# Four-layer hybrid network on one core: the last image's residual rows stay in SBUF, its positions and first norm go by halves, and 1/std is spread two chunks at a time

## The chip, the cores and the metric

The kernel runs on one core of a Trainium2 chip, in fp32. A core has five engines that run their own instruction streams in order: TensorE (PE, with its weight loads shown apart as PEld), VectorE (DVE), ScalarE (ACT), GpSimd (POOL) and SyncE (SP). They meet at semaphores. DMAs are issued from the queues of SP, ACT and POOL. The metric is the time of one execution on the device in microseconds; the median of several runs is compared.

## The reference

Four images of 96 channels and 64×64 pixels pass through four residual layers. Cut to what matters, with `_gn` a norm over groups of three channels, `_ln_t` a norm over the 96 channels of a pixel:

```python
x = x + layer0(_gn(x))        # norm, projection to 192+192 (x and gate z), 3x3 depthwise conv, silu,
                              # state-space scan over the 4096 pixels in four directions (rows, columns,
                              # each forwards and backwards), 16 states per channel;
                              # y = sum of the four; norm over 192; y*z; projection to 96
x = x + layer1(_gn(x))        # deformable 3x3 conv: a 3x3 conv gives 18 offsets and 9 masks per pixel,
                              # 9 taps are sampled bilinearly at base+offset, times the mask, then 96x96 each
t = t + fourier(_ln_t(t))     # 96 -> 192, relu, FFT over 4096 pixels, diagonal complex product, relu,
                              # inverse FFT, 192 -> 96
t = t + ffn(_ln_t(t))         # 96 -> 384 -> 96 with values rounded to short floats
t = t + linear_attention(_ln_t(t))
t = t + ffn(_ln_t(t))
```

## The kernel before

Images are worked on in order, and different layers of different images overlap. `Layer0.scan` is a list of 1536 scan units, 384 per image, in an order written out by hand. A unit covers 8 channels × 16 states on 128 partitions and 1024 pixels: ACT makes `da`, PE spreads the input into `db` (L1020), DVE multiplies and scans (L1034, L1042), POOL multiplies by `bc` (L1051), PE folds 128 rows into 32 (L1070). SP loads `du`, `bc` and stores `y`; ACT's queue loads `da`.

Between two units, the program is filled up with steps of two Python generators, called streams. `ends` holds `l0.first` and `l0.before(b)` (the inputs of the scans of each image) and then `l23.image(b)`, which is layers 2 and 3 of an image. `middle` holds, image by image, `l0.behind(b)` (out norm, gate and projection, giving x1) and `l1.image(b)` (layer 1, giving x2). Every step declares a cost per engine in microseconds; `Clock.has_room` lets a step in where the planned ends of the engines are not too far ahead, and `pipe` runs several chains of steps side by side, each when its tags (`takes`, `frees`) and PSUM banks (`has_bank`) allow. This happens while the program is built. On the chip each engine executes its instructions in the order in which the planner emitted them. Once the scan is over, `alone()` advances the planner's time by itself. `go()` steps both streams, `middle` first until the flag `sampling_last` is set, `ends` first from then on.

The parts that the change touches, for image b:

- `behind(b)`, L1092: for each pair of 512-pixel chunks from the last to the first, the sum of the column directions (`yta`, `ytc`, loaded transposed by halves of the image, L1112) and of the row directions, by POOL (L1134); centring and variance on PE; inverse root; spread of 1/std; gate by POOL (L1180); projection; x added (L1189) and x1 stored to DRAM.
- `offsets`, L1237: x1 loaded, `wom` loaded, group statistics (eight `bn_stats`, L448, then an aggregate and a small matmul), the normed image written by ACT, and copied by POOL into a padded tile `pad` (L1262); then 8 chunks, each with nine matmuls for the offsets (`po`, L1278), four transposes of the pixels (`pt`, L1295), copies (`pix`, `om`) and eight DMAs of 96 KB into a DRAM table (L1310) in which a row holds the four neighbours of a position.
- `positions`, L1319: loads `base`, then about 14 DVE operations of 288 or 576 columns give the row index `idx` and the four weights `wt` for all 288 × 128 taps.
- `sample`, L1366: 288 gathers (POOL, L1383), three to a tile `g`; they are weighted and summed by DVE (L1402, L1403) in the last image and by ACT (L1395) in the others; transposed (L1416), copied to `st` (L1424), multiplied by nine weight matrices (`pd`, L1432), x1 added (L1437), x2 stored to DRAM.
- `l23.image(b)`, L1819: loads x2 as `t`, and the Fourier layer begins with `normed` (L1603): `centred` (L470; chain per chunk, variance rows gathered in one bank, four rows per half), `inv_sqrt_steps`, and per chunk `spread` (L523), a matmul that copies one row of 1/std to all partitions, and a DVE product (L1613).

For the last image, layers 2 and 3 run halves of the image side by side where they can.

The last of these, the spread, reads:

```python
row = self.ident[:, j : j + 1].to_broadcast([128, 128])
self.nc.tensor.matmul(pb, lhsT=row, rhs=rstd, start=True, stop=True)
```

## Time and profile before

| what | us |
|---|---|
| median of three runs (8467.96 to 8479.75) | 8472.4 |
| the profiled execution | 8455.38 |
| its span, first to last instruction | 8453.6 |
| first and last scan on DVE start | 183.7, 7416.3 |
| last image: first gather starts | 7590.32 |
| last image: last row of x2 added, ends | 8036.3 |
| last image: first matmul of the Fourier layer | 8076.07 |
| image 2's output stored | 7905.2 |

The profiled execution is one of its own, 0.2% below the median of the runs. Times inside it are microseconds from the first instruction. The mean granted TensorE clock is 0.793 of full speed. Until 7418 the scan runs, with the other layers of earlier images between its units; what follows is the last image's way through the rest, beside the end of image 2. In a row of the timeline the bracket at the end gives the idle time of that engine ahead of the instruction and what ended it. A group's row gives its busy time, the mean of one, and the idle time before its instructions.

### The profile page before, as it was taken

To read this page: it belongs to the slowest core of one execution; us is meant where nothing else is said; L and a number is where in the kernel's file an instruction comes from. 1 tells how busy PE (TensorE), PEld (TensorE's weight loads), DVE (VectorE), ACT (ScalarE), POOL (GpSimd) and SP (SyncE) were. 2 spreads that over 40 slices of the span, in tenths; PEclk is the share of its full clock that TensorE was granted. 3 is DMA by queue.
4 is the path that set the end of the run, shared out by engine and by line. 5 is a ranking of instruction groups with operands and counts; after the bars stand their busy time and mean duration, and the time that the engine had idled before them with its cause. 6 is when DMAs were issued, how large, how long until landed. Compare 5 with 4: busy or idle time off the path is not lost.

```text
span 8453.6 us, 96209 instructions
## 1 busy us (share of the span) xinstructions
PE 6424.4 (76%) x31848; PEld 2772.6 (33%) x31848; DVE 6826.4 (81%) x5122; ACT 4914.8 (58%) x8979; POOL 5621.2 (66%) x4308
## 2 busy tenths in 40 slices
PE   6765787678766777977767889777788777797587
PEld 2211221112222223321222555222455232464273
DVE  2799889987789898779888898898898988838714
ACT  5665566555567777855566677645576876333224
POOL 1566566665568888856578898766798997627700
PEclk8776787678767778977667898786798787898698
DMA  3676678877679888877788999776899897744410
GB/s 98 169 209 186 166 190 214 204 186 188 171 205 241 233 235 220 230 187 198 194 216 233 236 237 245 184 177 175 224 239 235 216 228 188 187 111 138 142 60 17
DMA packets 773926, 1608.27 MB, mean 190 GB/s; under 512 B 264082, under 2 KB 355758, under 8 KB 771223
## 3 DMA queue, kind: packets, MB, share of 16 engines
q10 hardware_dynamic: 244224, 843.17, 39.2%
q1 hardware_dynamic: 455478, 532.37, 24.4%
q0 software_dynamic: 73728, 226.57, 10.1%
q8 instruction: 256, 4.19, 0.2%
q14 instruction: 240, 1.96, 0.1%
HBM read 1345.43 MB, written 256.29 MB: 189 GB/s over the span
## 4 chain that ended last, share of the span: by engine, by line
PE 32%; DVE 26%; DMA 12%; POOL 11%; issue 9%; ACT 8%; SPq 2%; ACTq 1%; DVEq 0%; POOLq 0%
DVE da L1042 12%; POOL da L1051 7%; DVE db L1034 7%; PE pc L763 3%; DMA da<-de 3%; PE py L1070 3%; PE ps L1416 3%; PE f L1510 3%; POOL g L1383 3%; PE pd L1432 2%; PE db L1020 2%; ACT g L1395 2%; ACT da L1014 2%; DMA du<-du 1%; PE h L1551 1%
## 5 line engine op out<-in xcount | busy, mean ns | idle before, releaser
L1051 POOL TENSOR_TENSOR da<-da,bc 128x1024 f32<-128x1024 f32 x1536 | 3664.1, 2387 | 351.6 <-DVE da L1042 233.3
L1042 DVE TENSOR_TENSOR_SCAN da<-da,st,db 128x1024 f32<-128x1024 f32 x1152 | 2701.1, 2345 | 124.1 <-ACT da L1014 12.8
L1034 DVE TENSOR_TENSOR db<-db,bc 128x1024 f32<-128x1024 f32 x1536 | 1865.4, 1214 | 614.7 <-PE db L1020 613.1
L1014 ACT ACTIVATE da<-da,w_al 128x1024 f32<-128x1024 f32 x1536 | 1737.7, 1146 | 405.7 <-DMA da<-de 166.9
L1383 POOL DMA_INDIRECT g<-table,idx x1152 | 1206.8, 1048 | 360.2 <-issue 178.7
L1020 PE MATMUL db<-du,rep 24*128 24x512 bf16 x3072 | 683.7, 450 | 774.4 <-DVE da L1042 729.0
L1070 PE MATMUL py<-da,w_fold 128*32 128x512 f32 x6144 | 1091.8, 784 | 43.6 <-issue 25.2
L1395 ACT ACTIVATE g<-g,wt 128x96 f32<-128x96 f32 x3456 | 964.0, 365 | 107.1 <-DMA g<-table,idx 18.4
L1042 DVE TENSOR_TENSOR_SCAN da<-da,db 128x1024 f32<-128x1024 f32 x384 | 877.0, 2284 | 54.7 <-ACT da L1014 19.6
L1416 PE MATMUL ps<-w_ident,g 128*96 128x128 f32 x3744 | 680.7, 325 | 252.3 <-issue 107.6
L1020 PEld LDWEIGHTS <-rep 24*128 24x128 bf16 x3072 | 147.3, 93 | 1839.2 <-DVE da L1042 1164.6
L851 POOL TENSOR_TENSOR lw<-lw,w 128x512 f32<-128x512 f32 x192 | 244.0, 1271 | 700.5 <-DVE w L849 667.8
L1416 PEld LDWEIGHTS ps<-w_ident,g 128*96 128x96 f32 x3744 | 483.5, 144 | 601.3 <-issue 178.9
L1049 POOL COPY st<-da 128x1 f32<-128x1 f32 x1152 | 232.2, 202 | 674.1 <-DVE da L1042 655.8
L763 PE MATMUL pc<-pad,wc 96*128 96x512 f32 x1152 | 576.3, 636 | 7.0 <-DVE rl L853 5.3
L1424 ACT COPY st<-ps 96x384 f32<-96x384 f32 x384 | 180.2, 472 | 572.3 <-PE ps L1416 533.8
L882 PE MATMUL pr<-ex,w_ident 128*128 128x512 f32 x384 | 311.2, 904 | 125.5 <-DVE ex L866 53.5
L1432 PE MATMUL pd<-st,wdc 96*128 96x256 f32 x1152 | 323.7, 434 | 12.7 <-DVE rl L853 6.0
L763 PEld LDWEIGHTS pc<-pad,wc 96*128 96x128 f32 x1152 | 217.9, 200 | 318.6 <-issue 303.5
L840 PE MATMUL pd<-xd,w_dtw 103*64 103x512 f32 (+1 forms) x512 | 273.4, 799 | 47.0 <-DVE rl L853 15.6
L1070 PEld LDWEIGHTS py<-da,w_fold 128*32 128x32 f32 x6144 | 158.1, 124 | 381.1 <-issue 300.3
L1432 PEld LDWEIGHTS pd<-st,wdc 96*128 96x128 f32 x1152 | 243.2, 219 | 104.2 <-issue 39.5
(259 smaller groups left out, 8631.4 us busy)
## 6 DMA issues: line engine op xcount, KB each, us to landing
da<-de ACTq DMA_DIRECT2D x1536, 512.0 KB
du<-du SPq DMA_DIRECT2D x1536, 96.0 KB
bc<-bcd SPq DMA_DIRECT2D x128, 512.0 KB
y<-yb SPq DMA_DIRECT2D x384, 128.0 KB
de<-rl SPq DMA_DIRECT2D x128, 256.0 KB
m<-in_dft SPq DMA_DIRECT2D x128, 256.0 KB
ad<-y ACTq DMA_DIRECT2D x192, 128.0 KB
table<-pix SPq DMA_DIRECT2D x256, 96.0 KB
```

What stands on the lines that cost most here:

```text
L763: nc.tensor.matmul(pp, lhsT=wc[:, q, g * 128 : (g + 1) * 128], rhs=pad[:, r0 + dy : r0 + dy + NR, dx : dx + W], start=(q == 0), stop=(q == 8),
L882: nc.tensor.matmul(pr, lhsT=net.ident, rhs=ex, start=True, stop=False)
L1014: self.net.nc.scalar.activation(u.da, u.da, AF.Exp, scale=self.al[:, a : a + 1])
L1020: self.net.nc.tensor.matmul(db[:, h, :], lhsT=self.rep[64 * u.q + 32 * h : 64 * u.q + 32 * h + 24], rhs=u.du[64 * u.q + 32 * h : 64 * u.q ...
L1034: self.net.nc.vector.tensor_mul(u.db, u.db, u.bc[:, 0, :])
L1042: nc.vector.tensor_tensor_scan(u.along(u.hh), u.along(u.da), u.along(u.db), first, ALU.mult, ALU.add)
L1051: self.net.nc.gpsimd.tensor_mul(u.hh, u.hh, u.bc[:, 1, :])
L1070: nc.tensor.matmul(py[p0 : p0 + 32], lhsT=self.fold[:, u.i, :], rhs=hc[:, h * CH : (h + 1) * CH], start=u.sums["add"] is None and u.i == 0 ...
L1383: nc.gpsimd.indirect_dma_start(out=g[:, k, :], out_offset=None, in_=self.tables[b % 2], in_offset=bass.IndirectOffsetOnAxis(ap=idx[:, n : ...
L1395: nc.scalar.activation(pixel, pixel, AF.Identity, scale=wt[:, n, c : c + 1])
L1416: nc.tensor.matmul(pt[:, k, :], lhsT=g[:, k, c * C : (c + 1) * C], rhs=net.ident, is_transpose=True, start=(c == 0), stop=(c == corners - 1),)
L1432: nc.tensor.matmul(po, lhsT=wdc[:, k, :], rhs=st[:, k, :], start=(k == 0), stop=(k == 8))
```

## The change

1. For the last image, x1 is a tile `x` in SBUF (pool `l1x`). It is loaded with the whole input image; `behind` adds to it in place and takes `bn_stats` of each chunk there. Neither the store of x1 nor its loads remain for this image. The transposed y is loaded by quarters of the image. In the very last pair of chunks, the sums and gate products are on DVE and no longer on POOL.
2. For all images, `offsets` lets ACT write the padded tile itself. The table comes first, in four chains `table(jj)` of 16 image rows each: 16 small matmuls against the identity from `pad`, two copies, eight DMAs of 192 KB. The eight chunks follow without transposes. For the last image the buffers are taken from the scan's ring of tiles (`ring`, `wide`).
3. `positions` takes a range of the taps. For the last image it runs twice on halves: the first after chunk 3 and the second as the first chain of `sample`; taps of the second half take the tag `half`.
4. `sample` of the last image adds to `x` in place, has `st` twice, and marks chunks in `net.arrived`; no x2 is stored or loaded.
5. The first norm of the last image's Fourier layer runs by halves, and its chains take `x{j}`, so that they can be emitted as the chunks arrive.
6. `spread` contracts over the 32 rows that hold the wanted one. `normed` and `normed_rows` issue the spreads of two chunks together.
7. `go()` tries `middle` first, and `ends` only if that one cannot step, whenever no scan unit paces the program (after the scan's end above all) and `sampling_last` is not yet set.

```diff
-            if chain.new and not net.has_bank():
+            if chain.new and not net.has_bank(int(chain.new)):
...
-            if not all(free[tag] > 0 for tag in chain.takes):
+            if not all(free.get(tag, net.arrived.get(tag, 0)) > 0 for tag in chain.takes):
...
-    def group_norm_stats(self, x, pool, key, stats):
+    def group_norm_stats(self, x, pool, key, stats, st=None):
 
         nc = self.nc
-        st = pool.tile([C, NCH, 6], F32, name=f"gnst{key}", tag="gnst")
-        for j in range(NCH):
-            nc.vector.bn_stats(st[:, j, :], x[:, j * CH : (j + 1) * CH])
-            if j % 2:
-                yield cost(dve=1.4)
+        if st is None:
+            st = pool.tile([C, NCH, 6], F32, name=f"gnst{key}", tag="gnst")
+            for j in range(NCH):
+                nc.vector.bn_stats(st[:, j, :], x[:, j * CH : (j + 1) * CH])
+                if j % 2:
...
-            yield wait(new=True, takes="sq")
+            yield wait(new=True, takes=f"sq x{j}" if arriving else "sq")
...
     def spread(self, rstd, j, n, key):
 
         pb = self.mm(f"lnb{key}_{j}")
-        row = self.ident[:, j : j + 1].to_broadcast([128, 128])
-        self.nc.tensor.matmul(pb, lhsT=row, rhs=rstd, start=True, stop=True)
+        k = slice(j - j % 32, j - j % 32 + 32)
+        row = self.ident[k, j : j + 1].to_broadcast([32, 128])
+        self.nc.tensor.matmul(pb, lhsT=row, rhs=rstd[k], start=True, stop=True)
         return pb[:n]
...
-                yield cost(pe=1.2, holds=1)
-                r = rows(pad, j)
-                nc.vector.tensor_mul(r, r, as_rows(pb))
-                yield cost(dve=0.7)
-                nc.scalar.activation(r, r, AF.Identity, scale=net.vec(V_ING, C), bias=net.vec(V_INB, C))
-                yield cost(act=0.8)
-
-            yield from pipe(self.net, (chain(j) for j in range(NCH)), 3)
+                yield wait(new=2)
+                pbs = [net.spread(rs, 32 * ((j + i) % 4) + (j + i) // 4, C, f"0_{b}") for i in range(2)]
+                yield cost(pe=1.2, holds=2)
+                for i in range(2):
+                    r = rows(pad, j + i)
+                    nc.vector.tensor_mul(r, r, as_rows(pbs[i]))
+                    yield cost(dve=0.7, holds=1 - i)
+                    nc.scalar.activation(r, r, AF.Identity, scale=net.vec(V_ING, C), bias=net.vec(V_INB, C))
+                    yield cost(act=0.8, holds=1 - i)
+
+            yield from pipe(self.net, (chain(j) for j in range(0, NCH, 2)), 2)
 
...
+    def ring(self, name, n, dtype=F32):
+
+        return self.sp.tile([128, T], dtype, name=name, tag="da", bufs=12)[:, :n]
+
+    def wide(self, name):
+        return self.sp.tile([128, 2, T], F32, name=name, tag="bc").rearrange("p s t -> p (s t)")
...
-                    ytc = big.tile([D2, W, H // 2], F32, name=f"ytc{b}_{h0}", tag="ytc")
+                rows = H // 2 if x1 is None else H // 4
+                if (j0 + HB) * NR % rows == 0:
+
+                    h0 = (j0 + HB) * NR - rows
+                    yta = big.tile([128, W, rows], F32, name=f"yta{b}_{h0}", tag="yta")
+                    ytc = big.tile([D2, W, rows], F32, name=f"ytc{b}_{h0}", tag="ytc")
                     for yt, c0 in ((yta, 0), (ytc, 128)):
                         src = self.y_d[b][3][c0 : c0 + yt.shape[0]].rearrange("c (w h) -> c w h", h=H)
-                        nc.sync.dma_start(yt, src[:, :, h0 : h0 + H // 2])
+                        nc.sync.dma_start(yt, src[:, :, h0 : h0 + rows])
                     yta_v, ytc_v = (t.rearrange("p w h -> p h w") for t in (yta, ytc))
                     yield wait(4.0)
                 while not all((b, 2, j * CH // T) in self.summed for j in range(j0, j0 + HB)):
                     yield BLOCKED
+                ends = b == B - 1 and j0 == 0
                 ca = big.tile([128, HB, CH], F32, name=f"ca{b}_{j0}", tag="ca")
                 cc = big.tile([D2, HB, CH], F32, name=f"cc{b}_{j0}", tag="cc")
                 net.hold(1)
...
-                    yield cost(pool=3.1, new=True)
+                        (nc.vector if ends else nc.gpsimd).tensor_add(y, y, yt[:, rs, :])
+                    yield cost(pool=3.1 * (not ends), dve=1.4 * ends, new=True)
                     for g, (o, c0, n) in enumerate(((ca, 0, 128), (cc, 128, D2))):
...
-                    yield cost(pool=2.6, new=True)
+                        (nc.vector if ends else nc.gpsimd).tensor_mul(o[:, i, :], o[:, i, :], z)
+                    if x1 is None:
+                        xr = op.tile([C, CH], F32, name=f"xr{b}_{j}", tag="xr")
+                        nc.sync.dma_start(xr, ins["x"][b][:, cs])
+                    else:
+                        xr = x1[:, cs]
+                    yield cost(pool=2.6 * (not ends), dve=1.4 * ends, new=True)
                     po = net.mm(f"po{b}_{j}")
                     nc.tensor.matmul(po, lhsT=wo_a, rhs=ca[:, i, :], start=True, stop=False)
...
                     yield cost(pe=1.3, holds=1)
                     nc.vector.tensor_add(xr, po[:C], xr)
-                    yield cost(dve=0.7)
-                    nc.sync.dma_start(self.x1[b][:, cs], xr)
-                    yield NOTHING
+                    if x1 is None:
+                        yield cost(dve=0.7)
+                        nc.sync.dma_start(self.x1[b][:, cs], xr)
+                        yield NOTHING
+                    else:
+                        nc.vector.bn_stats(st[:, j, :], xr)
+                        yield cost(dve=1.4)
...
+    def image(self, b, l0, ctx):
+
+        net = self.net
+        tc, nc = net.tc, net.nc
+        last = b == B - 1
+        if not last:
+            yield from l0.behind(b)
+        with ExitStack() as own:
+            if last:
+                kept = ctx.enter_context(tc.tile_pool(name=f"l1x{b}", bufs=1, side="right"))
+                x = kept.tile([C, L], F32, name=f"x1_{b}", tag="x")
+                st = kept.tile([C, NCH, 6], F32, name=f"gnst1_{b}", tag="gnst")
+                yield from l0.behind(b, x, st)
+            ix = own.enter_context(tc.tile_pool(name=f"l1i{b}", bufs=1, side="right"))
             idx = ix.tile([128, 288], U32, name=f"idx{b}", tag="idx")
             wt = ix.tile([128, 288, 4], F32, name=f"wt{b}", tag="wt")
...
+                def place_of(h):
+
+                    yield wait(takes=f"om{h}" if h == 0 else "")
+                    key = f"{b}_{h}"
...
+                    yield from self.positions(key, lambda name, *_: parts[name], om, base, idx, wt, 16 * h, 16)
+                    if h:
+                        net.arrived["half"] = 1
+
+                yield from self.offsets(b, x, st, om, place_of, l0)
+            else:
...
+            net.sampling_last = b == B - 1
+            if b == B - 1:
+                net.last_image = x
+            yield from self.sample(b, x, idx, wt, l0, place_of if last else None)
+        net.sampled.add(b)
...
+
             def filled(j):
-                cs = slice(j * CH, (j + 1) * CH)
-                nc.scalar.activation(x[:, cs], x[:, cs], AF.Identity, scale=rstd, bias=nmr)
+                nc.scalar.activation(Layer0.rows(pad, j), plain_rows(x, j), AF.Identity, scale=rstd, bias=nmr)
                 yield cost(act=0.8)
-                nc.gpsimd.tensor_copy(
-                    pad[:, 1 + j * NR : 1 + (j + 1) * NR, 1 : 1 + W],
-                    x[:, cs].rearrange("p (h w) -> p h w", w=W),
-                )
-                yield cost(pool=0.7)
-
-            yield from pipe(self.net, (filled(j) for j in range(NCH)), 2)
...
+            def table(jj):
+
+                yield wait(new=True, takes="pix")
+                if place_of is None:
+                    pix = pre.tile([128, 8, C], F32, name=f"pix{b}_{jj}", tag="pix")
+                else:
+                    pix = l0.ring(f"pix{b}_{jj}", 8 * C).rearrange("p (q c) -> p q c", c=C)
+                for h in range(2):
+                    pt = net.mm(f"pt{b}_{jj}_{h}")[:, : 4 * C].rearrange("p (q c) -> p q c", c=C)
+                    for q in range(4):
+                        for r in range(2):
+                            row = pad[:, 1 + 16 * jj + 8 * h + 2 * q + r, 1 : 1 + W]
+                            nc.tensor.matmul(
+                                pt[64 * r : 64 * r + 64, q, :],
+                                lhsT=row,
+                                rhs=net.ident[:C, :C],
+                                start=True,
+                                stop=True,
+                            )
+                    nc.scalar.copy(pix[:, 4 * h : 4 * h + 4, :], pt)
+                    yield cost(pe=0.9, act=0.5, new=h == 0)
+                for q in range(4):
+                    dy, dx = divmod(q, 2)
+                    for r in range(2):
+                        y0 = 2 + 16 * jj + r - dy
+                        dst = v[y0 : y0 + 15 : 2, 2 - dx : 2 - dx + W, q * C : (q + 1) * C]
+                        nc.sync.dma_start(dst.rearrange("t w d -> w t d"), pix[64 * r : 64 * r + 64])
+                yield wait(frees="pix")
 
             def chunk(j):
                 r0 = j * NR
+                yield wait(new=True, takes="po")
...
+            def chains():
+                for jj in range(NCH // 2):
+                    yield table(jj)
+                for j in range(NCH):
+                    yield chunk(j)
+                    if place_of is not None and j == 3:
+                        yield place_of(0)
+
+            yield from pipe(net, chains(), 4, every=-99, oc=min(deep, 2), pix=deep, po=min(deep, 2), om0=-3, om1=-3)
...
-                yield wait(takes="g")
+                yield wait(takes="g half" if last and t >= 16 else "g")
...
-                xr = gp.tile([C, 256], F32, name=f"xr1_{b}_{j}", tag="xr")
-                nc.sync.dma_start(xr, self.x1[b][:, cs])
+                if last:
+                    xr = xo = x[:, cs]
+                else:
...
-                nc.sync.dma_start(self.x2[b][:, cs], xo)
+                if not last:
+                    nc.sync.dma_start(self.x2[b][:, cs], xo)
+                elif j % 2:
+                    net.arrived[f"x{j // 2}"] = 1
...
-            yield from pipe(self.net, chains, 8, g=6, st=1, xo=1)
+            def chains():
+                if last:
+                    yield place_of(1)
+                for t in range(4 * NCH):
+                    for k0 in (0, 3, 6):
+                        yield taps(t, k0)
+
...
-                yield from normed(net, t, tl, f"2_{b}", pool)
+                if b == B - 1:
+                    for r in range(2):
+                        yield from normed(net, t, tl, f"2_{b}_{r}", pool, (r,), True)
+                else:
+                    yield from normed(net, t, tl, f"2_{b}", pool)
             tv = tl.rearrange("c (n1 n2) -> c n1 n2", n2=64)
...
+            if clock.own is not None and not net.sampling_last:
+                return any(stream.step() for stream in streams[::-1])
             return any([stream.step() for stream in (streams if net.sampling_last else streams[::-1])])
```

## Prediction

> **What bounds the kernel now.** I read the page's totals, the chain and the groups first. (Group rows: line, engine, operation, out<-in, count | busy us, mean ns | idle before, releaser.)
>
> ```profile
> span 8453.6 us, 96209 instructions
> ...
> PE 6424.4 (76%) x31848; PEld 2772.6 (33%) x31848; DVE 6826.4 (81%) x5122; ACT 4914.8 (58%) x8979; POOL 5621.2 (66%) x4308
> ...
> PE 32%; DVE 26%; DMA 12%; POOL 11%; issue 9%; ACT 8%; SPq 2%; ACTq 1%; DVEq 0%; POOLq 0%
> ...
> L1042 DVE TENSOR_TENSOR_SCAN da<-da,st,db 128x1024 f32<-128x1024 f32 x1152 | 2701.1, 2345 | 124.1 <-ACT da L1014 12.8
> L1034 DVE TENSOR_TENSOR db<-db,bc 128x1024 f32<-128x1024 f32 x1536 | 1865.4, 1214 | 614.7 <-PE db L1020 613.1
> ...
> L1383 POOL DMA_INDIRECT g<-table,idx x1152 | 1206.8, 1048 | 360.2 <-issue 178.7
> L1020 PE MATMUL db<-du,rep 24*128 24x512 bf16 x3072 | 683.7, 450 | 774.4 <-DVE da L1042 729.0
> ```
>
> No engine bounds the whole: the chain is spread over five. So I split the span by the timeline: 1536 scan units on DVE, 183.7 to 7418; then a tail of 1035 us. In the scan phase the two DVE operations need 1.21+2.35 = 3.6 us a unit, yet it advances at 4.5 to 4.9: other work and stalls. The tail by windows (busy us and count of PE, weight loads, DVE, ACT, POOL; granted clock; DMA share; GB/s):
>
> ```profile
> 7441.00:7481.00 40.00, 39.99 (x308) 25.46 (x308) 19.93 (x28) 9.33 (x15) 11.29 (x8) 1.00 0.19 53
> 7500.00:7590.00 90.00, 85.40 (x917) 67.12 (x915) 9.45 (x20) 36.22 (x72) 4.88 (x8) 0.96 0.53 121
> 7590.00:8025.00 435.00, 275.09 (x1031) 161.49 (x1030) 332.54 (x463) 114.03 (x233) 347.32 (x290) 0.74 0.49 144
> 8036.00:8076.00 40.00, 24.15 (x48) 8.58 (x48) 7.64 (x12) 10.19 (x19) 0.00 (x0) 0.74 0.17 42
> ```
>
> The last image's gathers cannot start before 7590.32, though PE is 95% busy before: that is image 2's Fourier layer, which nobody waits for yet. During sampling POOL is the fullest (347 of 435). In the last row nothing is full: a serial chain.
>
> **The change, part by part.** Sums are against the profiled execution, 8455.4 (span 8453.6); the runs' median 8472.4 lies 17.0 above it, which I add at the end.
>
> (a) Scan phase, images 0 to 2. The position arithmetic heads DVE's queue and waits for its base, whose load stands on SP behind the table's DMAs (the timelines of SP and DVE; columns: start, us, engine, instruction):
>
> ```profile
> 2375.50 5.23 SPq L1310 DMA_DIRECT2D table<-pix  x8
> ...
> 2383.00 0.35 SPq L393 DMA_DIRECT2D w_base<-in_base  x1
> ...
> 2386.28 0.76 DVE L1334 TENSOR_TENSOR pos<-om,w_base 128x576 f32<-128x576 f32 x1 [15.87 <-DMA w_base<-in_base]
> ```
>
> The same operation waits 12.68 us at 4235.70 (there a `du` load of the same queue is named, but the base is issued at 4232.54) and 10.39 at 5981.00: 38.9 in all. In the new order the table is issued 10 to 20 units ahead, so some 3.5 us of latency stays (SP 2383.00 to DVE 2386.28): 3×3.5 = 10.5, gain 28. The wait goes where? ACT's and PE's work for later units runs ahead meanwhile, so not all of the 28 need arrive. Against it: a table DMA now carries twice the bytes, 32 per image at the same total, and eight come together. With SP held 10.91 us by eight 96 KB issues at 4212.26, a batch costs at best nothing extra and at worst another 10.9; four batches in three images, bounds 0 and +131. I take +10, near the lower end: the bytes are equal. Image 3's transposed y now comes in four pairs of loads, not two:
>
> ```profile
> L1112 SPq DMA_DIRECT2D ytc<-y x8: 7970/12757/15796, 1604.8 to 7300.4; - x8
> ```
>
> (min/median/max ns). After such an issue the gap between scans was 6.9 to 20.9 us where 3.6 to 4.6 is normal. A quarter has the same number of packets at half the size, so SP is held as long; of four, one falls beside the last scan unit: one more stall, +10 (0 to +30). The whole x of image 3 (1.5 MB) is loaded there too, in place of eight small loads; a load of that size took 8.73 us at 8038, with nothing waiting for it here. ACT now fills the pad itself, 8×0.61 us of POOL less per image, off the path; the 64 small transposing matmuls for 32 (0.246 us each, before) add at most 8 us of PE per image, under a scan that DVE paces. The two streams' order moves by up to 12 units late in the scan, which reshuffles every small stall; I allow ±30. Sum −8, from −38 to +25 plus the 131 treated below as a rival.
>
> (b) Scan end to x1, 7441 to 7481: POOL's adds 4×1.55 and products 4×1.33, 11.5 us, become DVE's, 8×0.68 = 5.4 by the nearest product of 512 columns. Two chunks go side by side, so half of the 6.1 saved, 3, is on the chain; but PE is full (39.99 of 40), and image 2's matmuls stand between. I take 1.5 (0 to 5). Then the store and load of x1 (2.07), the weights behind them (8.92 DMA) and eight statistics (4.85), 16 us on the chain before the aggregate at 7497.4, go: x is in SBUF, statistics are taken per chunk, and the weights, first needed by the chunks, load beside the aggregate and the fill. Behind the aggregate, PE's queue held Fourier matmuls until 7509.4; now the chain's own come sooner. Pad filled 13 us earlier altogether, (b) included (8 to 16).
>
> (c) Pad to first gather, 7517.9 to 7590.3 = 72.4. Before: 64 table issues paced by PE and SP, 7528.4 to 7575.2, then the whole position arithmetic (7577 to 7589.5) behind the last chunk. Now: 32 issues of twice the size from deeper buffers, placed ahead of the chunks; the DMA engines were 0.73 busy over the 47 us, so they need at least 33 and take at most 43, from about 7508. The first positions follow chunk 3 and lie under these writes; the second half does too. Pad filled ≈7505, first table DMA 7508, first gather 7541 to 7551 plus a landing: ≈7547. Gain of (b) and (c) together 43 (33 to 52). Its price: image 2's Fourier, with 8 of 12 frequency blocks still to do, is pushed into sampling, some 66 us of PE.
>
> (d) Sampling, 434 us. PE has room, 435−275 = 160 us (the 66 at clock 0.96 are some 85 at the 0.74 of this row), but not at its start (31.46 of the first 36 already), where the whole push falls. The new conditions (half of the positions, chunk arrived) are tested while the program is built; on the chip they leave an order of instructions: the norm's centring stands in PE's queue behind the `pd` that it reads, the next triple's transposes stand behind it, and after six gather buffers POOL waits for those. DVE and POOL meet here: with DVE busy 20.6 to 23.4 us, 24 gathers took 34 to 35.5 us; with 32 to 34.7 they took 36.8 to 40. So a DVE us costs 0.2 to 0.4 us. New in this stretch: about 12 us of DVE of the pushed work and 5 of the first half of the norm (five to six operations of 0.7): 17×0.3 = 5; POOL's memset of the norm tile, 3.5; a few late PE answers in the first 90 gathers, 5. Sum +14 (3 to 40).
> A gather took 0.95 alone and up to 3.4 beside a DVE product. The Trainium skill ("SBUF — State Buffer", section on the two separate sides) holds that DVE and GpSimd share an exclusive port lock, so that the loser waits the whole operation out; by that rule the 17 us would cost up to 17 instead of 5, which speaks against loading DVE here. The windows' slope decides for me.
>
> (e) From the last sampled row to the Fourier layer, 39.8 us of plain chain:
>
> ```profile
> 8036.32 1.66 DMA x<-xo
> ...
> 8038.11 8.73 DMA t<-x
> 8046.88 7.02 PE lnc L485 x8
> ...
> 8065.56 9.65 PE lnb L527 x16
> ...
> 8076.07 3.94 PE h L1551 x50
> ```
>
> Store and load, 10.6, vanish. Of the norm's two halves the first (centring, variance, 4 us of root, spreads) lies under the sampling; the second's centring is done as chunks arrive but for the last one: about 2.5 centring, 1 variance, 4.1 root, 4 spreads and a product of 0.7, some 13 to 16 left. Gain 25 (20 to 28).
>
> (f) Spreads two chunks side by side: each took 0.593 at full clock and a pair 32 rows high may overlap, as L1020's 24-row pairs do (3072×0.450 = 1382 us in 683.7 busy). The three later norms spend 8.99, 4.29+3.67 and 8.83 us in spreads; pairs leave DVE's 0.68 product as the pace, 8×0.68 = 5.4 for 8.9. Gain 8 (0 to 14): 3.5+2+3.5 less a little.
> Against it stands the skill's "TensorEngine Tiling (Array Packing)", Key Properties: changing the tiling mode drains TensorE. No row here prices a drain; if each pair paid a few tenths, the 8 would shrink to about nothing.
>
> Sum: −8−43+14−25−8 = −70: profiled 8385, and with the 17 the median is **8402**.
>
> **Rivals.** B, *more*: the scan phase keeps its 28 without the two tens, sampling hides nearly everything, the ends come at their better bounds: −28−43+3−28−14 = −110, 8362. For it: DVE and PE are light in the last 130 us of sampling (DVE 20 to 23 of 35). Against: PE is full where the push falls.
> C, *sampling gives it back*: gathers that start 43 us sooner wait for PE's late transposes, or the sampling ends with image 2 still running: +45 in place of +14, so −39, 8433. For it: 31.46 of 36 us of PE busy at the start, and 66 more. Against: only the six gather buffers couple the two.
> D, *slower*: the doubled table DMAs hold up the scan's loads. SP issues in order, du, bc and de stand behind a batch on it, and the scan unit waits for them; if each of the 12 batches holds SP for twice 10.91 us and the scan waits that long, the 131 come in place of the 10: −70+121 = +51, 8523. It decides from 72 us of scan loss beyond (a)'s. For it: L1034's idle and the 13 us `ytc` issues, which did stop the scan. Against: equal bytes, and beside the batch at 4212.26 the scans went on at 4214.27 and 4218.25 until the base stopped them.
> E, *does not do what it says*: the planner's budgets keep the priority and the early half norm from moving anything, and only the removed copies and the base count: −8−16 (b) −10.6 (e) = −35, 8437. Against: the new program's order has half the norm ahead of the last gathers.
>
> **How the numbers follow.** Chances: forecast 0.50, B 0.16, C 0.16, D 0.10, E 0.08. A measurement of this kernel tells about 0.2%, 17 us. Adding the spreads of the terms as independent (30, 9, 18, 4, 7) gives ±37, so the forecast alone is 8365 to 8440. To leave no more than 2 in 10 out, the range takes in B, C and E with half of their own spread, 8350 to 8455; D stays outside. All but D centre on clearly faster; the upper edges of C and E reach within 17 us of before: faster 0.84, same 0.06, slower 0.10.
>
> **What would show it.** First gather some 130 us after the last scan's end (174 before); waits for w_base under 4 us on DVE before `pos`; at most 435+40 us from first to last gather; Fourier's `h` within 16 us of the last `xo`; spread groups under 6 us per eight. Wrong: the last scan unit later than 7450 (D), gathers still starting over 160 us after it (E), or sampling above 475 us (C).

## The result, and the profile after

The changed kernel is slower: 8538.8 us (median of 7 runs, 8520.2 to 8552.9) against 8485.3 for the kernel before in 7 runs beside and before it (8468.0 to 8507.1), a ratio of 1.0068 (95% interval 1.0049 to 1.0087). The profiled executions, 8541.85 and 8455.38, differ by 86.5 us. The medians differ by 53.5 only: the profiled execution of before is 30 us faster than the median of its runs, that of the changed kernel 3 us slower. So what the two profiles say of the loss is too large by some 33 us in all. The page after:

```profile
span 8540.1 us, 96714 instructions
...
PE 6551.0 (77%) x32232; PEld 2806.4 (33%) x32232; DVE 6833.4 (80%) x5149; ACT 4918.2 (58%) x8985; POOL 5595.1 (66%) x4268
```

DVE's work is the same to 7 us (6826.4 before), so the 86 us are waiting. Where they arose is told by cutting the span at the same events in both traces (us; first DVE scan to last scan, and then from the end of the last scan on):

| stage | before | after | difference | forecast |
|---|---|---|---|---|
| end of the last scan | 7418.7 | 7553.9 | +135.2 | −8 |
| from there to the last image's first gather | 171.6 | 114.1 | −57.6 | −43 |
| first to last gather | 434.4 | 481.8 | +47.4 | +14 |
| last gather to the end | 428.9 | 390.3 | −38.6 | −33 |

The last image's tail did what it should in two places, lost most of one gain in the sampling, and the scan phase, where hardly anything was meant to change, lost far more than all that. The scan phase of both kernels as one window each (columns as before: busy us and count of PE, weight loads, DVE, ACT, POOL; clock; DMA share; GB/s), first before:

```profile
186.03:7418.69 7232.66, 5512.08 (x25924) 2191.97 (x25927) 6275.55 (x4296) 4514.54 (x8263) 5235.03 (x3980) 0.78 0.81 207
```

and after, with the tail's stages:

```profile
187.47:7553.91 7366.44, 5654.90 (x25914) 2217.20 (x25914) 6284.28 (x4303) 4507.57 (x8252) 5225.53 (x3956) 0.75 0.79 203
7576.00:7668.00 92.00, 90.17 (x783) 56.06 (x783) 37.25 (x68) 33.04 (x59) 0.61 (x5) 1.00 0.44 121
7668.00:8150.00 482.00, 344.37 (x1978) 229.60 (x1976) 341.04 (x486) 147.69 (x296) 350.41 (x290) 0.76 0.44 132
```

The counts of instructions in the scan phase agree to 1%, and DVE is busy for 6275.6 and 6284.3 us; but it stands idle for 7232.7−6275.6 = 957 before and 1082 after. In the sampling, PE carries 344 us where it had 275: image 2's pushed work.

What DVE waited for in the scan phase, after (line that waits, releaser: us in total, times, longest us):

```profile
DVE db L1048 <- PE db L1034: 636.6, 328, 18.0
DVE t L1727 <- PE o L1725: 35.7, 7, 19.3
DVE xo L1554 <- DMA xr<-x: 25.0, 3, 10.8
...
DVE pos L1436 <- DMA du<-du: 3.3, 1, 3.3
```

The same view of before:

```profile
DVE db L1034 <- PE db L1020: 588.0, 310, 17.2
...
DVE pos L1334 <- DMA du<-du: 23.1, 2, 12.7
DVE pos L1334 <- DMA w_base<-in_base: 15.9, 1, 15.9
```

The wait for the base is gone, 39.0 to 3.3, as forecast. In its place stand other waits of the same kind: the scan's own input from PE (+49), the Fourier layer's result (5.3 to 35.7), and x1 for the sampling of an earlier image (no such row before).

### The profile page after: what moved, and what is told of

It is laid out like the page before. It is cut to its first block, busy times and chain, and to the rows that moved or that the text cites. A ratio compares the mean times of both kernels' runs of the same rounds, so it can differ in the third digit from the quotient of the medians.

```text
span 8540.1 us, 96714 instructions
## 1 busy us (share of the span) xinstructions
PE 6551.0 (77%) x32232; PEld 2806.4 (33%) x32232; DVE 6833.4 (80%) x5149; ACT 4918.2 (58%) x8985; POOL 5595.1 (66%) x4268
## 4 chain that ended last, share of the span: by engine, by line
PE 31%; DVE 27%; POOL 11%; DMA 11%; issue 9%; ACT 7%; SPq 1%; ACTq 1%; DVEq 0%; POOLq 0%; another core or an unknown queue 0%
DVE da L1056 12%; POOL da L1065 7%; DVE db L1048 7%; PE pc L770 4%; PE ps L1529 3%; PE f L1636 3%; PE py L1084 3%; POOL g L1496 2%; PE pd L1548 2%; PE db L1034 2%; DMA da<-de 2%; ACT g L1508 2%; ACT da L1028 1%; PE h L1681 1%; DMA m<-in_dft 1%
## 5 line engine op out<-in xcount | busy, mean ns | idle before, releaser
L1034 PE MATMUL db<-du,rep 24*128 24x512 bf16 x3072 | 707.5, 465 | 713.7 <-DVE da L1056 675.0
L1084 PE MATMUL py<-da,w_fold 128*32 128x512 f32 x6144 | 1148.0, 811 | 51.8 <-POOL da L1065 24.1
L1529 PE MATMUL ps<-w_ident,g 128*96 128x128 f32 x3744 | 699.5, 335 | 233.2 <-ACT g L1508 78.1
L1529 PEld LDWEIGHTS ps<-w_ident,g 128*96 128x96 f32 x3744 | 502.4, 148 | 590.0 <-ACT g L1508 202.2
L847 PE MATMUL pd<-xd,w_dtw 103*64 103x512 f32 (+1 forms) x512 | 281.8, 827 | 42.9 <-DVE rl L860 19.2
```

The costliest lines, as they stand in the source:

```text
L1034: self.net.nc.tensor.matmul(db[:, h, :], lhsT=self.rep[64 * u.q + 32 * h : 64 * u.q + 32 * h + 24], rhs=u.du[64 * u.q + 32 * h : 64 * u.q ...
L1084: nc.tensor.matmul(py[p0 : p0 + 32], lhsT=self.fold[:, u.i, :], rhs=hc[:, h * CH : (h + 1) * CH], start=u.sums["add"] is None and u.i == 0 ...
L1529: nc.tensor.matmul(pt[:, k, :], lhsT=g[:, k, c * C : (c + 1) * C], rhs=net.ident, is_transpose=True, start=(c == 0), stop=(c == corners - 1),)
```

## Experiments

All are edits of the changed kernel, and each run goes by the letter that the table gives it. "Scan end" is the end of the last scan in the profiled execution, "tail" what follows it; the ratio is to runs of the kernel before beside it.

| run | scan end | tail | time | ratio, 95% interval |
|---|---|---|---|---|
| before | 7418.7 | 1034.9 | 8485.3 | |
| after | 7553.9 | 986.2 | 8538.8 | 1.0068, 1.0049 to 1.0087 |
| d front and spread back | 7417.5 | 996.7 | 8449.1 | 0.9969, 0.9931 to 1.0006 |
| b front back | 7536.5 | 967.6 | 8498.8 | 1.0011, 0.9994 to 1.0027 |
| c spread back | 7519.9 | 1002.8 | 8526.9 | 1.0049, 1.0030 to 1.0067 |
| e no priority | 7542.7 | 1013.4 | 8577.0 | 1.0122, 1.0084 to 1.0160 |
| p1 32 rows, old order | 7455.0 | 997.2 | 8455.4 | 0.9971, 0.9956 to 0.9986 |
| p2 128 rows, pairs' order | 7535.6 | 977.7 | 8509.8 | 1.0039, 1.0021 to 1.0058 |
| n4 replanned, aggregate | 7476.5 | 995.8 | 8494.1 | 1.0015, 1.0000 to 1.0031 |
| n3 replanned, first norm | 7434.5 | 1004.6 | 8468.4 | 0.9967, 0.9947 to 0.9988 |
| n2 replanned, products | 7488.0 | 1003.6 | 8493.4 | one run |
| f pairs after the scan only | 7456.3 | 986.5 | 8445.0 | 0.9939, 0.9918 to 0.9961 |
| k3 f and base early | 7449.4 | 992.5 | 8432.9 | 0.9923, 0.9901 to 0.9945 |
| k2 f and gathers first | 7419.0 | 1101.2 | 8522.0 | one run |
| a1 change replanned | 7576.0 | 994.5 | 8572.3 | one run |
| a3 change replanned, first norm | 7509.9 | 1042.3 | 8554.0 | one run |
| b1 b replanned | 7572.2 | 992.4 | 8566.3 | one run |
| a4 96 KB table DMAs | 7618.0 | 999.8 | 8619.6 | one run |
| q1 pairs in first norms only | 7568.7 | 1002.8 | 8573.3 | one run |
| q2 pairs in later norms only | 7515.6 | 999.0 | 8516.4 | one run |

The scan phase of before's order was executed in five of these profiles (before, d, p1, f, k2): 7417.5 to 7456.3, mean 7433. This order is called the old order below, and scan ends are set against 7437, the mean of the first four. So one profile's scan end is good to about 20 us. A single run is good to less: the 18 runs of before beside d spread from 8438.2 to 8508.3, and the profile of d is the fastest of its five runs (8416.2, median 8449.1).

**Which part lengthens the scan.** d undoes the front of images 0 to 2 and the spreads, b the front alone, c the spreads alone.

```diff
# front back (d, b): in offsets, for images 0 to 2
+            if place_of is None:
+                yield from self.offsets_of_before(b, x, wom, pad, rstd, nmr, om, pre)
+                return
# spread back (d, c)
-        k = slice(j - j % 32, j - j % 32 + 32)
-        row = self.ident[k, j : j + 1].to_broadcast([32, 128])
-        self.nc.tensor.matmul(pb, lhsT=row, rhs=rstd[k], start=True, stop=True)
+        row = self.ident[:, j : j + 1].to_broadcast([128, 128])
+        self.nc.tensor.matmul(pb, lhsT=row, rhs=rstd, start=True, stop=True)
...
-    yield from pipe(net, (chain(js[n : n + 2]) for n in range(0, len(js), 2)), 2)
+    yield from pipe(net, (chain(j) for j in chunks(groups)), 3)
```

> Edit: the changed kernel with layer 1's front (pad by POOL, transposes in the chunks, 64 table DMAs of 96 KB) of images 0 to 2 and all spreads as before; only the last image's part of the change and the order after the scan remain. The emitted order up to image 3's `behind` is that of before. Theory (the new front of images 0 to 2, through the shifted order of the streams, cost the scan its 135 us): last scan at 7419 plus or minus 25, tail about 990, total about 8420. Rival 1 (the 32-row spreads slow PE): same here. Rival 2 (the chip's lower granted clock, not the change, made the scan longer): last scan at 7520 or later.

> Edit: the changed kernel with layer 1's front of images 0 to 2 as before; the paired 32-row spreads stay. Theory (front): scan end within 30 us of the kernel with both parts undone, total about 8420. Rival 1 (spreads): the scan keeps most of the 135, total about 8540.

> Edit: the changed kernel with full-height spreads, one chunk at a time, as before; the new front of images 0 to 2 stays. Theory (front): the scan still ends near 7554, and the three tail norms lose some 8 us, total about 8545. Rival 1 (spreads): scan end near 7420, total about 8415.

d: scan end 7417.5, tail 996.7: as expected. A slow chip (rival 2) is out as a cause: on the one chip on which both ran, d's granted clock is 0.790 and that of e, which keeps the whole order of the changed kernel's scan phase, 0.768 (medians of 5 and 4 runs). So the lower clock comes with the kernel. b and c were each to fall on one of two sides, and neither did: with the front undone, the scan still ends at 7536.5; with the spreads undone, at 7519.9. Either part alone costs 83 to 99 us against 7437, both together 117. Two independent prices would have added to some 180.

**Form or order.** p1 has the 32-row form without any instruction moved, p2 the pairs' order with the full form.

```diff
# p1: d, and in spread
+        k = slice(j - j % 32, j - j % 32 + 32)
+        row = self.ident[k, j : j + 1].to_broadcast([32, 128])
+        self.nc.tensor.matmul(pb, lhsT=row, rhs=rstd[k], start=True, stop=True)
# p2: b, and in spread
+        row = self.ident[:, j : j + 1].to_broadcast([128, 128])
+        self.nc.tensor.matmul(pb, lhsT=row, rhs=rstd, start=True, stop=True)
```

> Edit: the kernel with front and spreads undone, and now only the spread's contraction over 32 rows put back, one chunk at a time; not one instruction is moved against it. Theory (order: whatever moves the streams' steps among the scan units costs the scan about 100 us, the 32-row form itself nothing): last scan at 7417 plus or minus 30, total about 8445. Rival (form: matmuls over 32 rows among full ones slow PE or lower its clock): last scan at 7500 or later, mean clock near 0.777 where 0.795 was, total about 8500.

> Edit: the kernel with the front undone and paired 32-row spreads, with the spread's contraction over all 128 rows again; the pairs, and so the order, stay. Theory (order): last scan at 7530 plus or minus 30, as with 32 rows. Rival (form): last scan at 7440 or earlier and the clock back near 0.795.

For the pairs, order it is: 7455.0 and 7535.6. The first lies 8 us outside the stated ±30, but 45 short of what the rival asked. The times agree: 0.9971 of before for p1 (0.9956 to 0.9986) and 1.0039 for p2 (1.0021 to 1.0058). p1's mean clock is 0.776 (median of 8 runs) where d has 0.790, as the rival had it, and yet its time is d's; c and p2, at 0.788 and 0.787, have long scans. So the lower clock that the changed kernel shows is not what lengthens the scan either. For the front no such pair of runs was made: c's 83 us can be its order, or its own instructions. The scan phase of p2:

```profile
191.00:7535.55 7344.55, 5579.63 (x26020) 2230.18 (x26023) 6288.09 (x4308) 4521.74 (x8268) 5232.47 (x3980) 0.78 0.81 204
```

DVE is busy for 6288 us, 13 more than before, and idle for 7344.6−6288.1 = 1056.5, 99 more. The stalls are not noise: they fall at the same units where one order was executed twice. b and p2 share an order; so do the changed kernel and e, which has +17.3, −2.6, +23.0, +20.0 and +33.5 in the rows below. Time of 48 units in old order (mean of four, with the distance of highest and lowest), and what the others took beyond it, in rows with large losses (others are shorter than in the old order, down to −22.7 from unit 432 in the changed kernel):

| units from | old order | b | p2 | q1 | q2 | n4 | after |
|---|---|---|---|---|---|---|---|
| 624 | 204.0 (2.1) | +16.2 | +10.4 | +15.6 | +1.6 | +10.4 | +20.2 |
| 672 | 237.0 (2.5) | +27.4 | +28.1 | +24.4 | −1.0 | +5.5 | −10.7 |
| 912 | 204.6 (5.9) | +20.4 | +8.1 | +14.3 | +7.8 | +7.0 | +24.5 |
| 1104 | 219.1 (5.6) | +11.4 | +7.4 | +15.4 | +12.1 | +2.5 | +20.2 |
| 1200 | 205.6 (5.7) | +27.6 | +19.0 | −0.3 | +11.0 | +24.8 | +30.3 |

Most of the row at 672 can be read to its end. From unit 715 to 720, b takes 58.5 us and the old order (f) 38.6. The old order has one stall there, 18.9 us at unit 717; b has 25.8 at 716, 11.7 at 718 and 10.9 at 720. PE in the old order (f):

```profile
3656.84 2.07 PE L1155 MATMUL pc<-ya,w_cen_a 128*128 128x512 f32 x2 [16.70 <-POOL ya L1150]
3658.84 0.61 PE L1032 MATMUL db<-du,rep 24*128 24x512 bf16 x2
...
3677.35 1.96 PE L817 MATMUL px<-xa,w_xp_a 128*128 128x512 f32 x2
```

The timeline of SP in b:

```profile
3655.09 11.71 SPq L1129 DMA_DIRECT2D ytc<-y  x1
3666.84 3.96 SPq L1146 DMA_DIRECT2D ya<-y  x1
...
3675.85 0.34 SPq L396 DMA_DIRECT2D w_xp_a<-in_xp_a  x1
...
3677.04 5.20 SPq L1023 DMA_DIRECT2D du<-du  x4
```

and those of PE and DVE:

```profile
3679.56 2.04 PE L819 MATMUL px<-xa,w_xp_a 128*128 128x512 f32 x2 [24.31 <-DMA w_xp_a<-in_xp_a]
...
3683.54 0.61 PE L1034 MATMUL db<-du,rep 24*128 24x512 bf16 x2
```

```profile
3659.80 2.35 DVE L1056 TENSOR_TENSOR_SCAN da<-da,st,db 128x1024 f32<-128x1024 f32 x1 [0.49 <-DVE db L1048]
3684.19 1.23 DVE L1048 TENSOR_TENSOR db<-db,bc 128x1024 f32<-128x1024 f32 x1 [22.04 <-PE db L1034]
```

The load of a weight stands on SP behind the transposed y, whose issue alone holds SP for 11.71 us; the matmul that needs the weight stands on PE ahead of the scan unit's `db`; so DVE waits 22 us for a matmul of 0.61. Nothing in these queues is new: the old order's stall stands behind the same transposed y (there a sum of its rows, POOL's `ya`, is late). What the shift did is to put the matmul that needs the late weight ahead of the scan unit. In the old order it starts 20 us after PE's wait has ended and waits for nothing. At unit 718 of b, PE waits again, 6.75 us, for the weight issued next but one on SP (`w_dtw`).

Is any other order as bad? n4, n3 and n2 take d and alter one declared cost, so the planner lays the same instructions out otherwise.

```diff
# n4
         nc.vector.bn_aggr(mv, st)
-        yield cost(dve=0.4)
+        yield cost(dve=0.5)
# n3, n2: cost(dve=0.7) of the product behind the spread becomes 0.8, in the first norm and in layers 2 and 3
```

> Edit: the kernel with front and spreads undone, and one planning figure changed: the DVE cost that a group norm's aggregate declares is 0.5 in place of 0.4. The same instructions are issued with the same operands; from unit 157 their order among the scan units shifts, by up to 6 units on average in a stretch of 96. Theory (order is fitted): last scan 40 to 130 us later than 7417 though nothing is added. Rival (the change's own instructions cost the time): last scan within 25 us of 7417.

> Edit: the kernel with front and spreads undone, and another planning figure changed: the DVE cost of the first norm's product declared as 0.8 in place of 0.7. Same instructions, other order from unit 156 on. Theory (order is fitted): last scan 20 to 130 us later than 7437. Rival: within 20 us of it, or earlier.

> Edit: the kernel with front and spreads undone, and a third planning figure changed: the DVE cost of the product in layers 2 and 3's norms declared as 0.8 in place of 0.7. Same instructions, other order from unit 918 on. Theory (order is fitted): last scan 10 to 80 us later than 7437, the loss all behind unit 918. Rival: within 20 us of it, or earlier.

Scan ends 7476.5, 7434.5, 7488.0: against 7437, +40, −3 and +51 for nothing but an altered figure. n4's runs bear it out: 1.0015 of before (1.0000 to 1.0031), clear of p1's and n3's. n2 is a single run, with the loss where it was expected (3 us up to unit 918, 45 behind it); n3 missed my expectation. Then the changed orders replanned (a1, a3, b1 with the same figures), and the table DMAs halved (a4):

```diff
# a4
-                        y0 = 2 + 16 * jj + r - dy
-                        dst = v[y0 : y0 + 15 : 2, 2 - dx : 2 - dx + W, q * C : (q + 1) * C]
-                        nc.sync.dma_start(dst.rearrange("t w d -> w t d"), pix[64 * r : 64 * r + 64])
+                        for h in range(2):
+                            y0 = 2 + 16 * jj + 8 * h + r - dy
+                            dst = v[y0 : y0 + 7 : 2, 2 - dx : 2 - dx + W, q * C : (q + 1) * C]
...
```

> Edit: the changed kernel with one planning figure altered (the group norm aggregate's declared DVE cost 0.5 in place of 0.4). Same instructions, other order from unit 157. Draw: last scan anywhere from 7430 to 7560, and at least one of the three replanned kernels (this one, the first norm's product figure, the pairs alone) below 7490. Price of the change's parts: all three at 7510 or later.

> Edit: the changed kernel with another planning figure altered (the declared DVE cost of the first norm's product 0.8 in place of 0.7). Draw: as for the other, anywhere from 7430 to 7560. Price of the change's parts: 7510 or later.

> Edit: the kernel with the old front for images 0 to 2 and pairs everywhere, with the aggregate's declared DVE cost 0.5 in place of 0.4. Draw: last scan from 7430 to 7560 where 7536 was without the altered figure. Price of the pairs: 7510 or later.

> Edit: the changed kernel with each table DMA of 192 KB split into two of 96 KB at the same place; the order of all else is the same. Slower rival of the prediction (doubled DMAs hold SP and starve the scan): last scan 7500 or earlier. Theory (the size has no part): 7554 plus or minus 25; and the last image's first gather comes no more than 10 us later after the last scan than 114.

7576.0, 7509.9 and 7572.2: none below 7490, so "merely a bad draw" does not hold as I had put it; the changed orders scatter over 66 us and stay high, two of them beyond 7560 as well. a4 ends its scan at 7618.0, 64 us later than the changed kernel, with the first gather 127.4 us behind it, later than either side had it. That is one run, and e, with the same order, has a run of 8619.4 too; it does not speak for the doubled size. The issue times on SP speak against it. In the changed kernel eight table DMAs of 192 KB, issued together, hold SP for 6.8 to 9.2 us, where eight of 96 KB had held it for 5.2 to 10.9 before. With half as many of them, the table holds SP for 86.8 us of the scan phase in place of 126.4 (126.8 in a4).

q1 and q2 split the pairs between the norms, to see where their loss arises:

```diff
# q1: in normed (layers 2 and 3); q2: the same in normed_rows (first norm)
-        yield wait(new=2)
-        pbs = [net.spread(rs, 32 * (j % 4) + groups.index(j // 4), C, key) for j in js]
+        pb = net.spread(rs, 32 * (j % 4) + groups.index(j // 4), C, key)
```

> Edit: the kernel with the old front for images 0 to 2, 32-row spreads everywhere, in pairs only in the first norm of each image. If the loss is where loads collide after a small shift: scan units 576 to 768 cost 25 to 45 us more than in the old order, as with all pairs, and the last scan comes at 7470 to 7530. If the pairs of layers 2 and 3 alone cost the time: last scan 7437 plus or minus 25.

> Edit: the same, with pairs only in the norms of layers 2 and 3. The order is the old one up to unit 916. If the loss has two sources: units up to 900 within 15 us of the old order, then a loss of 20 to 60 us, last scan at 7460 to 7500. If the first norm's pairs alone cost it: last scan 7437 plus or minus 25.

q1: units 576 to 768 cost 31 us more, as foretold from the stall above, but the scan end of 7568.7 lies 39 beyond what I had allowed, and later than with all pairs. q2: 22 us up to unit 900, where 15 were allowed and where its order is still the old one (the old order's four executions lie between −10 and +18 of their mean there); then 7515.6, 16 beyond. The parts, +132 and +79 against 7437, do not add up to the +99 of both. A scan end belongs to an order as a whole.

**The sampling.** e takes the priority of the last image's chain away, k2 gives the gathers priority in the sampling too.

```diff
# e
-            if clock.own is not None and not net.sampling_last:
-                return any(stream.step() for stream in streams[::-1])
# k2 (on f)
-            return any([stream.step() for stream in (streams if net.sampling_last else streams[::-1])])
+            return any([stream.step() for stream in streams[::-1]])
```

> Edit: the changed kernel without the rule that steps `ends` only where `middle` cannot, after the scan. Theory (image 2's pushed Fourier work is what stretched the sampling from 434 to 482 us): the first gather comes 15 to 35 us later after the last scan than 114, the stretch from first to last gather shrinks by nearly as much to 450 or less, total within 20 us of the changed kernel. Rival (the half norm and DVE's added work stretch it): first gather later, sampling still 475 or more, total 20 to 40 us longer.

> Edit: the kernel with the old front for images 0 to 2 and pairs after the scan only, with `middle` stepped first during the last sampling too. Image 2's layers 2 and 3 are put off behind the gathers, so the total is expected longer. Theory (the sampling is stretched because transposes stand behind image 2's Fourier matmuls on PE, and POOL runs out of its six gather buffers): POOL waits under 8 us for `ps` where it waited 36, and the 288 gathers take 425 to 445 us where they took 474 to 478. Rival (the added DVE and norm work stretches it): over 460.

What POOL waited for between the first and the last gather, in the changed kernel:

```profile
POOL g L1496 <- issue: 63.7, 210, 0.3
...
POOL g L1496 <- PE ps L1529: 44.4, 12, 25.3
```

in the kernel before, where the 63.7 of "issue" are the same:

```profile
POOL g L1383 <- PE ps L1416: 1.5, 5, 0.3
```

and in k2:

```profile
POOL g L1556 <- PE ps L1589: 15.9, 9, 6.7
```

The 44.4 − 1.5 = 42.9 us are nearly the whole stretch of 47.4. The gathers themselves did not grow: the 288 take 343.6 us together before and 343.4 after. The longest of these waits on the timelines of PE and POOL, after:

```profile
7762.18 19.89 PE L1636 MATMUL f<-w_idft,d 128*64 128x64 f32 x320
7782.00 2.41 PE L1529 MATMUL ps<-w_ident,g 128*96 128x128 f32 x18
```

```profile
7782.80 0.94 POOL L1496 DMA_INDIRECT g<-table,idx  x1 [25.35 <-PE ps L1529]
```

20 us of image 2's Fourier matmuls stand ahead of 18 transposes, six tiles of three: all the gather buffers there are. k2 puts that work off, and its gathers take 550.5−118.9 = 431.6 us, as the theory said, though 15.9 us of waits for `ps` remained where I had expected under 8. Its total is longer, since image 2 then runs after the gathers. k2 takes work off DVE too (265 us of it in the stretch, where f has 341), so it does not tell the two alone; but DVE's work in the stretch had hardly grown with the change, from 333 to 341. e missed, and its numbers are the rival's: its first gather comes 11 us later, its sampling takes 496.9, its total is 38 us longer. Without the priority the same Fourier work still stands there (PE 351 us in it, and POOL waits 36.8 for `ps`); in e POOL also waits 22.9 us for DVE's `x` and `g`, so there the rival has a part. In the kernel before, image 2 had 172 us ahead of the first gather and in e only 125.

**What can be kept.** f uses pairs only after the scan's end; k3 also loads the base early.

```diff
# f
-        k = slice(j - j % 32, j - j % 32 + 32)
+        k = slice(0, 128) if self.own_banks is None else slice(j - j % 32, j - j % 32 + 32)
...
+    if net.own_banks is None:
+        yield from pipe(net, (chain(j) for j in js), 3)
+    else:
+        yield from pipe(net, (pair(js[n : n + 2]) for n in range(0, len(js), 2)), 2)
# k3
+                    base = wt.rearrange("p n c -> p (n c)")[:, :576].rearrange("p (s n) -> p s n", s=2)
+                    nc.sync.dma_start(base, net.ins["base"])
...
-                        base = net.load("base", pp)
```

> Edit: the kernel with front and spreads undone, with paired 32-row spreads only where the norm is emitted after the scan's end. The order up to the scan's end is that of before. Theory (order, or form inside the scan): last scan at 7417 plus or minus 25; tail 965 to 985 where 997 was; total about 8425, faster than before by 0.5 to 1.0%. Rival (pairs do not help the tail): tail 990 to 1000, total 8449.

> Edit: the kernel with the old front for images 0 to 2 and pairs after the scan only, with the position arithmetic's base loaded at the beginning of the front (into the tile that will hold the weights) and no longer behind the table's DMAs; 58 instructions of 42,000 move. Theory (the base wait is a real stall of DVE and can be had without a new order): no wait for the base over 1 us before `pos`, the three waits of 39 us together gone, last scan 15 to 40 us before 7437 (the mean of four executions of that order), total 0.8 to 1.2% below before. Rival (the wait only takes the place of one that follows, so nothing arrives): last scan 7437 plus or minus 15.

f has the gain expected, with a tail of 986.5 for d's 996.7 and 0.9939 (0.9918 to 0.9961) in all; its tail is 1.5 above the stated bound and its scan end of 7456.3 lies 14 outside the ±25. k3 missed in its reason: `pos` still waited 28.4 us where it waited 42.4 in f, now with a table DMA named for 16.2 and `bcd` for 12.2, and the scan ended at 7449.4, no earlier than the old order's. Its 0.9923 (0.9901 to 0.9945) is not told from f's. Both beat both kernels.

## Why the prediction was wrong

(a) is the step that failed: "The two streams' order moves by up to 12 units late in the scan, which reshuffles every small stall; I allow ±30." The term was −8 and measured +135 in the two profiles, 117 against the mean of the old order, and about 100 by the medians (the changed kernel's 8538.8 against d's 8449.1, with tails 10 us apart). Three errors lie in it. The order moved not late but early: in the traces DVE's instructions of the other layers stand within a unit of their old place up to unit 422, and from 480 on they lie 9 to 35 units off on average in each stretch of 96. The allowance was taken as symmetrical, but eleven other orders of the scan phase came out at −3 to +139 us against 7437, and not one clearly earlier: among these the old order is a favourable one. And a shift is not small: one matmul put ahead of a scan unit cost 22 us at unit 716. Its parts: the base wait went as forecast (39 to 3.3), but k3, which takes part of it away without a new order, shows no gain in the scan end, so the 28 us were not seen to arrive even by themselves; the transposed y of image 3 in four loads (43.5 us of SP in the changed kernel, where two loads held it for 25.6 before) is within d's 7417.5 too and cost nothing visible.

The sign came from rival D, the size too (131), but its mechanism was wrong: b loses 99 us without any doubled DMA in its scan phase, and the doubled ones hold SP for less time in all, not for twice as long (86.8 us against 126.4). That D's number came out is luck. What D had right is that loads standing on SP behind long issues can stop the scan, as at unit 716; there the issue is a transposed y that before has as well.

(b) and (c), first gather: −43 forecast, −57.6 measured. The mechanism held, and the table in larger DMAs ahead of the chunks took even less: 25.0 us from its first issue to its last (7635.2 to 7660.2), where 33 to 43 were foreseen.

(d), sampling: +14 forecast, +47.4 measured. Here rival C came true, with its mechanism (PE's late transposes behind pushed work) and its size (+45). The term "a few late PE answers in the first 90 gathers, 5" measured 42.9. By C the first gather's gain is worth 10 of its 57.6 us at the last gather: 606.1 before, 595.9 after, counted from the scan's end. The Trainium skill's rule on DVE and GpSimd ("SBUF — State Buffer", the section on two separate sides) was not needed for it: by that rule the gathers would grow or start late beside DVE, and they are as long as before (343.4 and 343.6 us in sum) and wait as little for DVE ("DVE g", 7.0 us in 23 waits of 0.3, and 7.6 in 25 before).

(e), last sampled row to the Fourier layer: −25 forecast, −28.1 measured (39.8 to 11.7). The chain of waits after:

```profile
8162.11 0.49 DVE x L1554
8162.60 0.04 issue
8162.65 1.12 PE lnc L489 x2
8163.77 1.74 PE lnv L505 x8
...
8169.58 2.16 PE lnb L532 x8
8171.74 2.52 issue
8174.26 19.15 PE h L1681 x256
```

No store, no load, a centring of two instructions: what was forecast, in order.

(f), spreads in pairs: −8 forecast. From the first to the last spread of the later norms: 11.15, 6.01, 3.67 and 10.99 us before, 7.38, 1.14, 3.02 and 6.95 after, 13.3 less; four spreads went through in 1.14. f, which has the pairs behind the scan alone, has a tail 10.2 shorter than d's. (The 0.593 of the forecast is one of two matmul records of a spread, so half of one.) "TensorEngine Tiling (Array Packing)", Key Properties, speaks of a drain at each change of mode; p1 has 252 such matmuls in its scan phase, among full ones, at d's time, so no cost of a drain is seen here. Two times that are good to some 30 us could hide 0.1 us for each.

The tail's terms together, −62 forecast, came to −48.7. So the forecast of the tail was fair, and the order of the scan decided.

What stays open: why the changed orders all lie 73 us or more behind the old one, while orders replanned from the old lie 51 or less behind. That the old order's planning figures were fitted to it would give that, and so would a price of the new parts that acts only through order; a1, a3 and b1 do not tell these apart. PE's waits for DMAs in the scan phase (66 to 95 us in the old order, 138 in b, 175 in q1, but 94 in the changed kernel and 145 in n3, which lost nothing) don't account for it alone. Whether the new front's own instructions cost part of c's 83 us was not tested either. Most of these scan ends are single profiles.

## To carry to other kernels

Where a build-time planner lays many streams out around a hand-ordered loop, any edit that it sees is also a new order, and the order may be worth more than the edit: measure an edit with the order held fixed, and a new order without the edit. Confine a tail change to the tail (f, with what the change does for the last image: 0.6% faster; the whole change: 0.7% slower). A stage that starts earlier pulls its competitor's work into itself; count the gain at that stage's end, not at its start.

## What the runs showed of the hardware

With the spreads over 32 rows and nothing moved, the mean granted TensorE clock is 0.776 in place of 0.790 (medians of 8 and 5 runs), at the same time (8455.4 and 8449.1): here the mean clock of a run does not tell its time. Spreads of 32 rows from different row groups overlap well: the first matmuls of four start within 0.02 us of each other, and the four went through in 1.14 us, where four of the old form took 3.67 in the same norm. Executions of one and the same order differ by up to 39 us over the scan phase (7417.5 to 7456.3), yet its stalls fall on the same units: of 48 units in the five rows above, the four executions differ by 2.1 to 5.9 us.
